# A state-space scan, an attention and an expert layer on one core: the product with B in two halves, the product with C behind a semaphore, the last columns on VectorE, the gate on y's banks, and a new order of the work

## The chip, the cores and the metric

The kernel runs on one core of a Trainium2 chip. The metric is the device time of one execution in microseconds; the median of several runs is given. Engines are called PE (TensorE), DVE (VectorE), ACT (ScalarE), POOL (GpSimd) and SP (SyncE, which here only issues DMAs).

## The reference

The input `x` has 16 images of 128 channels and 64 x 64 pixels. Layer 0 is a group norm, then a selective state-space block over the 4096 tokens of an image with 256 inner channels and 16 states, and a residual. Layer 1 is a causal softmax-weighted attention with one query per head (8 heads), and then a layer of 64 experts that each choose 8 tokens. The change touches layer 0 and, in small things, the attention's scores. Cut to what matters:

```python
u = x.transpose(0, 2, 3, 1).reshape(b, h * w, c)
xs, z = jnp.split(u @ W_in, 2, axis=-1)
xc = silu(causal_depthwise_conv4(xs) + conv_b)
dt, Bm, Cm = jnp.split(xc @ W_xproj, [DT_RANK, DT_RANK + D_STATE], axis=-1)
delta = softplus(dt @ W_dt + b_dt);  A = -exp(A_log)
def step(hs, inp):
    d_t, B_t, C_t, u_t = inp
    h_new = exp(d_t[:, :, None] * A) * hs + (d_t * u_t)[:, :, None] * B_t[:, None, :]
    y_t = einsum('bdn,bn->bd', h_new, C_t)
    return h_new, y_t
y = (scan(step) + xc * D_param) * silu(z)
out = y @ W_out
# attention: s = q . silu(k);  exp(s - cummax(s)), its running sum u, the running sum w of exp(...) * silu(v);  w / u, mean of heads
```

## The kernel before

**Tiling.** Channels lie on the 128 partitions, tokens along the free dimension. An image is cut into 8 blocks of 512 tokens, so there are 128 blocks. The 256 inner channels are two halves `a` of 128 partitions; a tile such as `h` is 128 x 2 x 512 in fp32. One loop over `k` runs the scan of block `k`, the preparation of block `k + 1` (norm, convolution, projections, `delta`), the closing of block `k - 1` (gate, output projection, residual) and the attention of block `k - 9`, all interleaved. After the loop come ten rounds with attention alone, then the choice of tokens, the experts, and a last pass that adds their outputs.

**The state loop.** In block `k` there is one step for each state `n` from 0 to 15:

- `product` (line 379): DVE multiplies `du` (delta times the convolved input) by row B of `bct`, a tile in which both rows (B and C) of this state are spread over all partitions by a DMA on SP three steps earlier. The result `bx` (128 x 1024) is in PSUM, in one tile with one buffer.
- `scan` (line 385): two `tensor_tensor_scan` on DVE, one for each half, read the decay `da` (made by ACT ahead of time) and `bx` and write `h`; the start value is the kept `state` of the block before. Then POOL multiplies `h` by row C and writes over `da`.
- `keep_state` (line 406): POOL copies the last column of both halves of `h` (two elements per partition) to `state`, except in an image's last block.
- `add_pair` (line 401): for n = 1, 3, 5, 7 POOL issues a DMA that adds the `da` of the state before into this one.
- `add_y` (line 412): PE transposes `da` and accumulates it in `y` (two PSUM banks, one buffer) with tokens on partitions.

**The closing of a block.** `take_y` has ACT copy `y` to SBUF, `turn_y` has PE turn it back to channels on partitions (`yb`), `gate` has DVE multiply it with `z`, and `out_proj` has PE multiply by `wo`.

**Order.** Every engine works through its instructions in program order (`InOrder`, line 22). The interleaving is written out by hand: `STEP` (line 724) has for each `n` three strings of short names, and `do(n, part)` (line 831) issues them: part 0 after `product`, part 1 between the two scans (through `between`), part 2 after the state is kept. A `d` issues one decay. `ge0` to `ge4` are the parts of `gn_end` (line 258), which ends the group norm's statistics of the next image; `less` is `score_less` (line 533), six small DVE operations on the attention's scores; `gate0` and `gate1`, `takey`, `turny`, `outp`, `put` close the block; `du` makes `delta_x` of the next block; `ar0` to `ar3` and `sr0` to `sr3` add the residual by DMAs on POOL and store it by DMAs on SP.

Of the kernel before, what the change touches and what calls it, by code (L numbers as in the profile page):

```python
# [17 lines left out]
NEG = -3.0e38  # L18
OFF = -1.0e30
EXP_LN = "natural_log_exp_and_others"  # L20


class InOrder:
# [16 lines left out]
def conv_attn_hybrid(ctx: ExitStack, tc: tile.TileContext, x, w_in, conv_w, conv_b, w_xproj, w_dt, b_dt,  # L40
# [41 lines left out]
    with ExitStack() as st:  # L82
# [175 lines left out]
        def gn_end(b, part):  # L258

            w = gn[b]  # L260
            if part == 0:
                w["mv"] = stp.tile([P, 2], F32, tag="mv", name="mv")
                w["gs"] = stp.tile([P, 5], F32, tag="gs", name="gs")
                DVE.bn_aggr(w["mv"], w["stats"].rearrange("p a b -> p (a b)"))
            mv, gs = w["mv"], w["gs"]
            if part == 1:
                w["gp"] = bank("gn_ps")
                PE.matmul(w["gp"][:, 0:1], gmat, mv[:, 0:1], start=True, stop=True)
                ACT.copy(gs[:, 0:1], w["gp"][:, 0:1])
            if part == 2:  # L270
                DVE.tensor_tensor(gs[:, 1:2], mv[:, 0:1], gs[:, 0:1], ALU.subtract)
                DVE.scalar_tensor_tensor(gs[:, 1:2], gs[:, 1:2], gs[:, 1:2], mv[:, 1:2], ALU.mult, ALU.add)
            if part == 3:
                w["gp"] = bank("gn_ps2")
                PE.matmul(w["gp"][:, 0:1], gmat, gs[:, 1:2], start=True, stop=True)
                ACT.activation(gs[:, 2:3], w["gp"][:, 0:1], AF.Ln, bias=eps)
                ACT.activation(gs[:, 3:4], gs[:, 2:3], AF.Exp, scale=-0.5)
            if part == 4:
                DVE.tensor_scalar(gs[:, 4:5], gs[:, 0:1], gs[:, 3:4], -1.0, ALU.mult, ALU.mult)
# [35 lines left out]
                ACT.activation(xc[:, a, :], w[f"xs{a}"], AF.Silu, bias=cb[:, a : a + 1])  # L315

        def gate_silu(k):
            w = blocks[k]
            z = w["z"] = m1.tile([P, NH2, L], F32, tag="z", name="z")
            for a in range(NH2):  # L320
                pt = bank("z_ps")
                PE.matmul(pt, wz[:, bass.ts(a, P)], w["xb"][:, KC - 1 :], start=True, stop=True)
                ACT.activation(z[:, a, :], pt, AF.Silu)

        def xproj(k):

# [52 lines left out]
        def product(k, n):  # L379

            w = blocks[k]
            bx = w["bx"] = bps.tile([P, NH2, L], F32, tag="bx", name="bx")
            DVE.tensor_tensor(bx, w["du"], bc(w["bc", n][:, 0:1, :], [P, NH2, L]), ALU.mult)

        def scan(k, n, between):


            w = blocks[k]
            b, i = w["b"], w["i"]
            if n == 0 and i == 0:  # L390
                gn[b]["state"] = stp.tile([P, N, NH2], F32, tag="state", name="state")
            bt, da, bx = w.pop(("bc", n)), w["da", n], w.pop("bx")
            h = w["h", n] = hp_.tile([P, NH2, L], F32, tag="h", name="h")
            for a in range(NH2):
                if a:
                    between(n)
                DVE.tensor_tensor_scan(h[:, a, :], da[:, a, :], bx[:, a, :],
                                       0.0 if i == 0 else gn[b]["state"][:, n, a : a + 1], ALU.mult, ALU.add)
            POOL.tensor_tensor(da, h, bc(bt[:, 1:2, :], [P, NH2, L]), ALU.mult)

        def add_pair(k, n):

# [3 lines left out]
        def keep_state(k, n):  # L406
            w = blocks[k]
            h = w.pop(("h", n))
            if w["i"] < NBLK - 1:
                POOL.tensor_copy(gn[w["b"]]["state"][:, n, :], h[:, :, L - 1])  # L410

        def add_y(k, n):

# [11 lines left out]
                              is_transpose=True, skip_group_check=True)  # L425


        def take_y(k):
            w = blocks[k]
            yt = w["yt"] = a1.tile([P, L // P, DI], F32, tag="wm", name="yt", bufs=2)  # L430
            for c in range(0, L // P, 2):
                ACT.copy(yt[:, c : c + 2, :], w["y"][:, c : c + 2, :])

        def turn_y(k):
            w = blocks[k]
            for a in range(NH2):
                yb = w[f"yb{a}"] = bank("yb_ps")
                for c in range(L // P):
                    PE.transpose(yb[:, bass.ts(c, P)], w["yt"][:, c, bass.ts(a, P)], ident)

        def gate(k, a):
            w = blocks[k]
            DVE.tensor_tensor(w["z"][:, a, :], w[f"yb{a}"], w["z"][:, a, :], ALU.mult)

        def tokens_of(w):

# [3 lines left out]
        def out_proj(k):  # L450

            w = blocks[k]
            w["o"] = bank("o_ps")
            for a in range(NH2):
                PE.matmul(w["o"], wo[:, a, :], w["z"][:, a, :], start=(a == 0), stop=(a == NH2 - 1))

        def add_residual(b, part):

# [3 lines left out]
                POOL.dma_start(res[b][:, to], x_f[b, :, to], accum_op=ALU.add)  # L462

        def store_residual(b, part):
            SP.dma_start(t1_d[b, :, bass.ts(part, T // 4)], res[b][:, bass.ts(part, T // 4)])

        def put_back(k):
            w = blocks.pop(k)
# [61 lines left out]
            s["mx"] = a1.tile([P, 64], F32, tag="mx", name="mx")  # L530
            DVE.tensor_tensor_scan(s["mx"], bc(negc, [P, 64]), s["s"][:, :64], NEG, ALU.max, ALU.max)

        def score_less(m):


            i = m % NBLK
            s = att[m]
            mx, z = s.pop("mx"), s["s"][:, 64:P]
            DVE.transpose(z[:, 32:], mx[:, 32:])
            if i == 0:  # L540
                DVE.memset(z[:, 0:48:47], NEG)
            else:
                DVE.tensor_copy(z[:, 0:48:47], zl)
            DVE.tensor_tensor_scan(z[:, 1:32], open_, z[:, 32:63], z[:, 0:1], ALU.min, ALU.max)
            DVE.tensor_copy(zl, z[:, NC8 : NC8 + 17 : 16])
            back = stp.tile([P, 32], F32, tag="back", name="back")
            DVE.transpose(back, z[:, :32])
            s["x2"] = a1.tile([P, 2, 64], F32, tag="x2", name="x2")
            DVE.scalar_tensor_tensor(s["x2"][:, 0, :], mx, back[:, 31:32], s["s"][:, :64], ALU.max, ALU.subtract)

        def score_exp(m):
            s = att[m]
# [161 lines left out]
        def finish(m, f):  # L714
# [7 lines left out]
        PAIRS = (1, 3, 5, 7)  # L722
        LEAD, LEAD_BC = 8, 3
        STEP = (
            ("lx0 k0 k4 yp14", "yp15", "takey k1 k2"),
            ("k3 v6", "norm skip", "tu0 fin0"),
            ("", "k5", "ge0 s0 k6 turny ge1 k7"),
            ("s1", "gate0", ""),
            ("v4 v7 ge2 gate1 v5 mx d d y-1 conv0", "d less y1", "sexp"),
            ("w1 a10 a11 exp d ts1", "ge3 outp d put tsc ssp c1 d", ""),  # L730
            ("", "", "conv1"),
            ("ar0 ssum ar1 b1 d slog rest1 ar2 split1 y3 to1 rest2 d conv2 csilu", "split2", "d store v0"),
            ("tu1 lx1 v2 ge4", "fin1 cen", ""),
            ("", "", ""),
            ("v1 xproj v3 z delta sq exp bcs", "var", "lnsc"),
            ("", "y5 y7", "spread inv w0 d"),
            ("gnl a00 a01", "y8", "d y9 lb ar3 sr0"),
            ("sr1 d y10 y11 ts0 d", "c0 y12", ""),
            ("b0", "", "sr2"),
            ("d lnap gns", "du", "nt d d sr3 y13 d d to0"),  # L740
        )
        order = [(k, n) for k in range(NK) for n in range(N)]
        made = 0
# [35 lines left out]
        for k in range(NK + LAG + 1):  # L779
# [11 lines left out]
            ops = dict(  # L791
                norm=(nxt, norm_block), conv0=(nxt, lambda k: conv(k, 0)), conv1=(nxt, lambda k: conv(k, 1, range(KC // 2))),
                conv2=(nxt, lambda k: conv(k, 1, range(KC // 2, KC))), csilu=(nxt, conv_silu), xproj=(nxt, xproj),
                bcs=(nxt, store_bc), delta=(nxt, delta), du=(nxt, delta_x), z=(cur, gate_silu), skip=(cur, skip),
                takey=(prev, take_y), turny=(prev, turn_y), gate0=(prev, lambda k: gate(k, 0)),
                gate1=(prev, lambda k: gate(k, 1)), outp=(prev, out_proj), put=(prev, put_back),
                cen=(mn, ln_center), sq=(mn, ln_square), var=(mn, ln_var), lnsc=(mn, ln_scale), lnap=(mn, ln_apply),
                mx=(m, score_max), less=(m, score_less), sexp=(m, score_exp), tsc=(m, turn_scores), ssum=(m, score_sum),
                ssp=(m, spread_scores), slog=(m, score_log), rest1=(m, lambda m: rest(m, 1)), split1=(m, lambda m: split(m, 1)),
                rest2=(m, lambda m: rest(m, 2)), split2=(m, lambda m: split(m, 2)), store=(m, store_parts),  # L800
                spread=(m, spread_parts), inv=(m, inverse), lx0=(mn, lambda m: load_x(m, True)), lx1=(m, load_x),
                gnl=(stat, lambda s: gn_load(*s)), gns=(stat, lambda s: gn_stats(*s)),
                lb=(k + 2 if k + 2 < NK else None, lambda k: load_block(k, ACT)),
                nt=(k + 2 if k + 2 < NK else None, no_tokens), exp=(0, lambda _: load_exp()))
            for h in range(HD):
# [13 lines left out]
            for f in range(2):  # L819
                ops[f"tu{f}"] = (mp_, lambda m, f=f: turn_o(m, f))  # L820
                ops[f"fin{f}"] = (mp_, lambda m, f=f: finish(m, f))
            for n in range(-1, N):
                ops[f"y{n}"] = (cur, lambda k, n=n: add_y(k, n))
                ops[f"yp{n}"] = (prev, lambda k, n=n: add_y(k, n))
# [13 lines left out]
                        f(of)  # L838

            for n in range(N):  # L840
                if cur is not None:
                    product(cur, n)
                do(n, 0)
                if cur is not None:
                    later = k * N + n + LEAD_BC
                    if later < NK * N:
                        load_bc(*order[later])
                    scan(cur, n, lambda n: do(n, 1))
                    keep_state(cur, n)
                    if n in PAIRS:  # L850
                        add_pair(cur, n)
                else:
                    do(n, 1)
                do(n, 2)
# [292 lines left out]
```

## Time and profile before

| | |
|---|---|
| median of 3 runs | 9924.13 us (9919.84 to 9943.96) |
| profiled execution | 9941.12 us, its span 9939.4 us |
| busy in the span | PE 86%, DVE 88%, ACT 74%, POOL 73%, PE weight loads 51% |
| scans on DVE | 4096, together 5022 us |
| products with B on DVE | 2048, 2621 us, mean 1280 ns |
| products with C on POOL | 2048, 6626 us, mean 3240 ns |
| copies of the last columns on POOL | 1792, 432 us |

The profile is of one execution. Times in it are microseconds unless ns is said. A line of the timeline has start, duration, engine, the line of the code, operation, names and shapes (out<-in), and how many in a row. All engines but PE share one line, 31, because a helper issues their work, so groups are told apart by the names of their tiles. A busy share is an average over the whole span; the scan stage runs from about 50 us to 8680 us.

### The profile page before, as it was taken

To read this page: it belongs to the slowest core of one execution; us is meant where nothing else is said; L and a number is where in the kernel's file an instruction comes from. 1 tells how busy PE (TensorE), PEld (TensorE's weight loads), DVE (VectorE), ACT (ScalarE), POOL (GpSimd) and SP (SyncE) were. 2 spreads that over 40 slices of the span, in tenths; PEclk is the share of its full clock that TensorE was granted. 3 is DMA by queue.
4 is the path that set the end of the run, shared out by engine and by line. 5 is a ranking of instruction groups with operands and counts; after the bars stand their busy time and mean duration, and the time that the engine had idled before them with its cause. 6 is when DMAs were issued, how large, how long until landed. Compare 5 with 4: busy or idle time off the path is not lost.

```text
span 9939.4 us, 183919 instructions
## 1 busy us (share of the span) xinstructions
PE 8516.5 (86%) x69084; PEld 5113.5 (51%) x69084; DVE 8709.0 (88%) x9217; ACT 7385.9 (74%) x14079; POOL 7301.8 (73%) x4475
## 2 busy tenths in 40 slices
PE   5579898998989898989999898989898998877775
PEld 3345555555555555555555555555555555545642
DVE  8999999999999999999999999999999999902743
ACT  4568787888878887878878788878788887755730
POOL 7888888888888888888888888888888888800000
PEclk7789999999999999999999999999999999998976
DMA  6677777777776777777777777777777777611358
GB/s 164 173 188 181 189 185 190 183 179 192 181 194 176 197 181 189 182 191 180 186 190 177 194 181 193 180 194 178 194 181 192 183 178 186 163 38 55 119 169 352
DMA packets 978014, 1783.42 MB, mean 179 GB/s; under 512 B 194953, under 2 KB 275489, under 8 KB 967905
## 3 DMA queue, kind: packets, MB, share of 16 engines
q1 hardware_dynamic: 724480, 1381.32, 50.1%
q0 software_dynamic: 82944, 302.03, 15.4%
q10 hardware_dynamic: 169696, 88.30, 3.1%
q8 instruction: 544, 8.91, 0.3%
q14 instruction: 350, 2.86, 0.1%
HBM read 1363.99 MB, written 138.94 MB: 151 GB/s over the span
## 4 chain that ended last, share of the span: by engine, by line
PE 45%; ACT 34%; DVE 9%; DMA 6%; issue 5%; ACTq 1%; SPq 0%; POOL 0%; DVEq 0%; POOLq 0%
ACT da L31 11%; PE ao_ps L31 9%; PE v_ps L31 9%; PE y_ps L31 6%; ACT L31 6%; PE k_ps L31 4%; DVE h L31 3%; DVE bx L31 3%; PE o_ps L31 2%; PE z_ps L31 2%; ACT xc L31 2%; PE xs_ps L31 2%; PE var_ps L31 2%; ACT kt L31 2%; DMA bct<-bcs 2%
## 5 line engine op out<-in xcount | busy, mean ns | idle before, releaser
L31 POOL TENSOR_TENSOR da<-h,bct 128x1024 f32<-128x1024 f32 x2048 | 6626.3, 3240 | 1275.8 <-DVE h L31 667.0
L31 DVE TENSOR_TENSOR_SCAN h<-da,state,bx 128x512 f32<-128x512 f32 x3584 | 4420.8, 1267 | 201.6 <-DVE bx L31 4.3
L31 DVE TENSOR_TENSOR bx<-du,bct 128x1024 f32<-128x1024 f32 x2048 | 2621.4, 1280 | 115.0 <-DMA bct<-bcs 45.8
L31 ACT ACTIVATE da<-delta,a_neg 128x512 f32<-128x512 f32 x4096 | 2621.8, 714 | 27.9 <-DMA da<-da 17.2
L31 PE MATMUL y_ps<-ident,da 128*128 128x128 f32 x12288 | 1708.5, 296 | 236.6 <-POOL da L31 124.5
L31 PEld LDWEIGHTS y_ps<-ident,da 128*128 128x128 f32 x12288 | 1559.7, 154 | 540.8 <-issue 256.3
L31 PE MATMUL v_ps<-wv,xn 128*64 128x512 f32 x4096 | 1074.6, 624 | 200.3 <-ACT xc L31 134.9
L31 ACT ACTIVATE v<-v_ps 128x512 f32<-128x512 f32 x1024 | 610.8, 598 | 790.6 <-PE v_ps L31 790.0
L31 PE MATMUL k_ps<-xn,wk 128*128 128x512 f32 x2048 | 1038.7, 613 | 97.6 <-ACT kt L31 93.1
L31 PE MATMUL xs_ps<-xb,wc 128*128 128x512 f32 x2048 | 975.7, 609 | 23.7 <-ACT xt L31 4.2
L31 ACT ACTIVATE kt<-k_ps 128x512 f32<-128x512 f32 x1024 | 565.6, 612 | 234.2 <-PE k_ps L31 165.0
L31 PE MATMUL ao_ps<-v,wm 128*64 128x128 f32 x8192 | 580.4, 286 | 151.9 <-ACT wm L31 150.7
L31 ACT ACT_TABLE_LOAD x526 | 674.9, 1283 | 14.1 <-ACT parts L31 4.4
L31 DVE TENSOR_TENSOR_SCAN h<-da,bx 128x512 f32<-128x512 f32 x512 | 600.8, 1208 | 32.5 <-POOL state L31 3.0
L31 PEld LDWEIGHTS v_ps<-wv,xn 128*64 128x64 f32 x4096 | 228.5, 137 | 745.6 <-ACT xc L31 232.4
L31 PEld LDWEIGHTS ao_ps<-v,wm 128*64 128x64 f32 x8192 | 453.8, 140 | 267.4 <-ACT wm L31 213.5
L31 PEld LDWEIGHTS xs_ps<-xb,wc 128*128 128x128 f32 x2048 | 366.0, 193 | 368.8 <-issue 321.7
L31 POOL DMA_DIRECT2D da<-da x512 | 460.0, 899 | 98.4 <-POOL state L31 65.4
L31 PEld LDWEIGHTS k_ps<-xn,wk 128*128 128x128 f32 x2048 | 331.2, 190 | 349.4 <-ACT kt L31 215.6
L31 PE MATMUL var_ps<-sq,mean_w 128*128 128x512 f32 x256 | 219.6, 953 | 277.8 <-ACT sq L31 277.8
L31 POOL COPY state<-h 128x2 f32<-128x2 f32 x1792 | 432.4, 241 | 0.0
L31 PEld LDWEIGHTS s_ps<-kt,q 128*32 128x32 f32 x16384 | 257.2, 110 | 271.6 <-issue 97.8
(209 smaller groups left out, 10326.6 us busy)
## 6 DMA issues: line engine op xcount, KB each, us to landing
bct<-bcs SPq DMA_DIRECT2D x2048, 512.0 KB
da<-da POOLq DMA_DIRECT2D x512, 512.0 KB, 7.9
xs<-t_d SPq DMA_DIRECT2D x240, 256.0 KB
xs<-in_x_dram SPq DMA_DIRECT2D x128, 256.0 KB
t_d<-xt SPq DMA_DIRECT2D x64, 512.0 KB
t_d<-tx ACTq DMA_DIRECT2D x256, 128.0 KB
t<-t_d SPq DMA_DIRECT2D x128, 256.0 KB
tc<-t_d SPq DMA_DIRECT2D x16, 2048.0 KB
```

What stands on the lines that cost most here:

```text
L31: return lambda *args, **kw: self.tc.keep_in_program_order(f(*args, **kw))
```

## The change

- `product` writes two PSUM tiles `bx0` and `bx1` with two DVE instructions of 128 x 512.
- The product with C and the pair's DMA leave `scan`; a new function `product_c` issues them in the next step, after that step's `product`, and makes POOL wait by a semaphore for that step's first half (in the last step of a block, for its second half, behind which `delta_x` of the next block is issued at once).
- `keep_state` runs there too, on DVE in place of POOL.
- The gate multiplies `y` in PSUM, tokens on partitions, with a `z` that is now made with tokens on partitions; only then PE turns the result and ACT copies it out (`gy`), and `out_proj` reads `gy`.
- In part 2 of `gn_end` the intermediate value lies in PSUM (`far`).
- `score_less` comes in six parts `l0` to `l5`. The residual's stores are issued on ACT's queue. `STEP` is new.

```diff
+def after(tc, ins, other):
+    tc.add_manual_dep(ins.ins, other.ins.name,
+                      mybir.DependencyInfo(mybir.DependencyClass.Sync, mybir.DependencyReason.DATA), reason="port")
 def gn_end(b, part):
             if part == 2:
-                DVE.tensor_tensor(gs[:, 1:2], mv[:, 0:1], gs[:, 0:1], ALU.subtract)
-                DVE.scalar_tensor_tensor(gs[:, 1:2], gs[:, 1:2], gs[:, 1:2], mv[:, 1:2], ALU.mult, ALU.add)
+                far = w["gp"][:, 1:2]
+                DVE.tensor_tensor(far, mv[:, 0:1], w["gp"][:, 0:1], ALU.subtract)
+                DVE.scalar_tensor_tensor(gs[:, 1:2], far, far, mv[:, 1:2], ALU.mult, ALU.add)
...
 def gate_silu(k):
-            z = w["z"] = m1.tile([P, NH2, L], F32, tag="z", name="z")
-            for a in range(NH2):
+            z = w["z"] = m1.tile([P, L // P, DI], F32, tag="z", name="z")
+            for q in range(2):
                 pt = bank("z_ps")
-                PE.matmul(pt, wz[:, bass.ts(a, P)], w["xb"][:, KC - 1 :], start=True, stop=True)
-                ACT.activation(z[:, a, :], pt, AF.Silu)
+                for c in range(2):
+                    at = KC - 1 + (2 * q + c) * P
+                    PE.matmul(pt[:, bass.ts(c, DI)], w["xb"][:, at : at + P], wz, start=True, stop=True)
+                ACT.activation(z[:, 2 * q : 2 * q + 2, :].rearrange("p c d -> p (c d)"), pt, AF.Silu)
...
 def product(k, n):
-            bx = w["bx"] = bps.tile([P, NH2, L], F32, tag="bx", name="bx")
-            DVE.tensor_tensor(bx, w["du"], bc(w["bc", n][:, 0:1, :], [P, NH2, L]), ALU.mult)
+            bx = w["bx"] = [bps.tile([P, L], F32, tag=f"bx{a}", name=f"bx{a}") for a in range(NH2)]
+            for a in range(NH2):
+                w["bxi", a] = DVE.tensor_tensor(bx[a], w["du"][:, a, :], w["bc", n][:, 0, :], ALU.mult)
...
-            POOL.tensor_tensor(da, h, bc(bt[:, 1:2, :], [P, NH2, L]), ALU.mult)
+            w["hc", n] = bt
+        def product_c(k, n, behind):
+            w = blocks[k]
+            bt = w.pop(("hc", n))
+            ins = POOL.tensor_tensor(w["da", n], w["h", n], bc(bt[:, 1:2, :], [P, NH2, L]), ALU.mult)
+            if behind is not None:
+                after(tc, ins, behind)
+            if n in PAIRS:
+                add_pair(k, n)
...
-                POOL.tensor_copy(gn[w["b"]]["state"][:, n, :], h[:, :, L - 1])
+                DVE.tensor_copy(gn[w["b"]]["state"][:, n, :], h[:, :, L - 1])
...
-        def take_y(k):
-        def gate(k, a):
-            DVE.tensor_tensor(w["z"][:, a, :], w[f"yb{a}"], w["z"][:, a, :], ALU.mult)
+        def gate(k, q):
+            cs = slice(2 * q, 2 * q + 2)
+            DVE.tensor_tensor(w["z"][:, cs, :], w["y"][:, cs, :], w["z"][:, cs, :], ALU.mult)
+        def turn_y(k, a):
+            if a == 0:
+                w["gy"] = a1.tile([P, NH2, L], F32, tag="wm", name="gy", bufs=2)
+            yb = bank("yb_ps")
+            for c in range(L // P):
+                PE.transpose(yb[:, bass.ts(c, P)], w["z"][:, c, bass.ts(a, P)], ident)
+            ACT.copy(w["gy"][:, a, :], yb)
...
-            SP.dma_start(t1_d[b, :, bass.ts(part, T // 4)], res[b][:, bass.ts(part, T // 4)])
+            ACT.dma_start(t1_d[b, :, bass.ts(part, T // 4)], res[b][:, bass.ts(part, T // 4)])
...
+            ("yp14 yp15 k4 ge0 k0", "", "k1 k2"),
+            ("k3", "k5", ""),
+            ("norm tu0 g0 ge1 g1 fin0", "", "s0 v6 k6 k7"),
+            ("", "", "ty0 s1 ty1 skip"),
+            ("v7 v4 lx0 mx v5 exp y-1 l1 d d ge2 l0", "y1 w1 d d l2 l4 l3 l5", "conv0"),
+            ("d sexp d d ge3 a10 outp a11", "", "tsc"),
+            ("ssp y3", "", "put ts1"),
+            ("ssum slog conv1 rest1 d d c1 split1 conv2 rest2 csilu", "split2", "d b1"),
+            ("", "ar0 lx1 store z v2 to1 xproj v0 tu1", ""),
+            ("", "ge4 ar1 bcs v3", ""),
+            ("cen fin1 sq v1 delta var exp lnsc y5 ar2", "", ""),
+            ("inv", "", "ar3 spread"),
+            ("sr0 d y7 y8 w0 d d", "a00", "y9 d"),
+            ("a01 ts0 lb y10", "sr1 y11 d", "c0"),
+            ("d sr2 gnl la", "nt d y12", ""),
+            ("y13 b0", "gs", "sr3 d to0"),
...
             for n in range(N):
+                behind = None
                 if cur is not None:
                     product(cur, n)
+                    behind = blocks[cur]["bxi", 0]
+                    if n == N - 1 and nxt is not None:
+                        behind = blocks[cur]["bxi", 1]
+                        delta_x(nxt)
+                if 0 < k * N + n <= NK * N:
+                    product_c(*divmod(k * N + n - 1, N), behind)
+                    keep_state(*divmod(k * N + n - 1, N))
                 do(n, 0)
...
                     scan(cur, n, lambda n: do(n, 1))
-                    keep_state(cur, n)
-                    if n in PAIRS:
-                        add_pair(cur, n)
```

More of the change, by code (lines that the diff above doesn't have):

```diff
@@ L396, in scan @@
                     between(n)
-                DVE.tensor_tensor_scan(h[:, a, :], da[:, a, :], bx[:, a, :],
+                DVE.tensor_tensor_scan(h[:, a, :], da[:, a, :], bx[a],
                                        0.0 if i == 0 else gn[b]["state"][:, n, a : a + 1], ALU.mult, ALU.add)
-            POOL.tensor_tensor(da, h, bc(bt[:, 1:2, :], [P, NH2, L]), ALU.mult)
+            w["hc", n] = bt
[7 more added lines that the diff above has]
+                add_pair(k, n)
         def add_pair(k, n):
@@ L425, in add_y @@
                               is_transpose=True, skip_group_check=True)
-        def take_y(k):
+        def gate(k, q):
             w = blocks[k]
[L430 to L434, printed above, removed]
+            cs = slice(2 * q, 2 * q + 2)
+            DVE.tensor_tensor(w["z"][:, cs, :], w["y"][:, cs, :], w["z"][:, cs, :], ALU.mult)
+        def turn_y(k, a):
             w = blocks[k]
[L436 to L439, printed above, removed]
-        def gate(k, a):
-            w = blocks[k]
-            DVE.tensor_tensor(w["z"][:, a, :], w[f"yb{a}"], w["z"][:, a, :], ALU.mult)
+            if a == 0:
[4 more added lines that the diff above has]
+            ACT.copy(w["gy"][:, a, :], yb)
         def tokens_of(w):
@@ L454, in out_proj @@
             for a in range(NH2):
-                PE.matmul(w["o"], wo[:, a, :], w["z"][:, a, :], start=(a == 0), stop=(a == NH2 - 1))
+                PE.matmul(w["o"], wo[:, a, :], w["gy"][:, a, :], start=(a == 0), stop=(a == NH2 - 1))
         def add_residual(b, part):
@@ L531, in score_max, with score_less @@
             DVE.tensor_tensor_scan(s["mx"], bc(negc, [P, 64]), s["s"][:, :64], NEG, ALU.max, ALU.max)
-        def score_less(m):
+        def score_less(m, part):
             i = m % NBLK
             s = att[m]
[L538 to L549, printed above, removed]
+            mx, z = s["mx"], s["s"][:, 64:P]
+            if part == 0:
+                DVE.transpose(z[:, 32:], mx[:, 32:])
+            if part == 1:
+                if i == 0:
+                    DVE.memset(z[:, 0:48:47], NEG)
+                else:
+                    DVE.tensor_copy(z[:, 0:48:47], zl)
+            if part == 2:
+                DVE.tensor_tensor_scan(z[:, 1:32], open_, z[:, 32:63], z[:, 0:1], ALU.min, ALU.max)
+            if part == 3:
+                DVE.tensor_copy(zl, z[:, NC8 : NC8 + 17 : 16])
+            if part == 4:
+                s["back"] = stp.tile([P, 32], F32, tag="back", name="back")
+                DVE.transpose(s["back"], z[:, :32])
+            if part == 5:
+                s["x2"] = a1.tile([P, 2, 64], F32, tag="x2", name="x2")
+                DVE.scalar_tensor_tensor(s["x2"][:, 0, :], mx, s["back"][:, 31:32], s["s"][:, :64], ALU.max, ALU.subtract)
         def score_exp(m):
@@ L724, in conv_attn_hybrid @@
         STEP = (
[L725 to L740, printed above, removed]
+            ("yp14 yp15 k4 ge0 k0", "", "k1 k2"),
[10 more added lines that the diff above has]
+            ("inv", "", "ar3 spread"),
[4 rows of a table added]
         )
@@ L793, in conv_attn_hybrid @@
                 conv2=(nxt, lambda k: conv(k, 1, range(KC // 2, KC))), csilu=(nxt, conv_silu), xproj=(nxt, xproj),
[L794 to L798, printed above, removed]
+                bcs=(nxt, store_bc), delta=(nxt, delta), z=(cur, gate_silu), skip=(cur, skip),
+                outp=(prev, out_proj), put=(prev, put_back),
+                cen=(mn, ln_center), sq=(mn, ln_square), var=(mn, ln_var), lnsc=(mn, ln_scale),
+                mx=(m, score_max), sexp=(m, score_exp), tsc=(m, turn_scores), ssum=(m, score_sum),
                 ssp=(m, spread_scores), slog=(m, score_log), rest1=(m, lambda m: rest(m, 1)), split1=(m, lambda m: split(m, 1)),
@@ L801, in conv_attn_hybrid @@
                 spread=(m, spread_parts), inv=(m, inverse), lx0=(mn, lambda m: load_x(m, True)), lx1=(m, load_x),
-                gnl=(stat, lambda s: gn_load(*s)), gns=(stat, lambda s: gn_stats(*s)),
+                gnl=(stat, lambda s: gn_load(*s)),
                 lb=(k + 2 if k + 2 < NK else None, lambda k: load_block(k, ACT)),
@@ L821, in conv_attn_hybrid @@
                 ops[f"fin{f}"] = (mp_, lambda m, f=f: finish(m, f))
+            for q in range(2):
+                ops[f"g{q}"] = (prev, lambda k, q=q: gate(k, q))
+            for a in range(NH2):
+                ops[f"ty{a}"] = (prev, lambda k, a=a: turn_y(k, a))
+            ops["la"] = (mn, ln_apply)
+            ops["gs"] = (stat, lambda s: gn_stats(*s))
+            for part in range(6):
+                ops[f"l{part}"] = (m, lambda m, part=part: score_less(m, part))
             for n in range(-1, N):
```

## The prediction

> **What bounds the kernel now.** I read the page's busy table first, then the slices of busy time, then the timeline of VectorE (DVE) and GpSimd (POOL) in one steady block, then single tiles.
>
> ```profile
> PE 8516.5 (86%) x69084; PEld 5113.5 (51%) x69084; DVE 8709.0 (88%) x9217; ACT 7385.9 (74%) x14079; POOL 7301.8 (73%) x4475
> DVE  8999999999999999999999999999999999902743
> 4019.18:4085.28 66.10, 60.23 (x501) 35.51 (x500) 63.19 (x60) 54.67 (x103) 56.56 (x36) 0.95 0.72 181
> ```
>
> The third line is one block of 512 tokens (window, its length, then busy us of PE, weight loads, DVE, ACT, POOL): DVE 63.19 of 66.10 us. Across 1000 to 8000 us it is 6675 of 7000. The scan stage lasts to 8.7 ms, so DVE's instruction starts, added up, are the time. The chain of waits names PE and ACT (45% and 34%), but it ran last through the attention tail after 8.7 ms; in the stage DVE hardly waits for them.
>
> A plain step of the state loop (start, duration, DVE):
>
> ```profile
> 4056.87 1.23 DVE L31 TENSOR_TENSOR bx<-du,bct 128x1024 f32<-128x1024 f32 x1
> 4058.24 2.45 DVE L31 TENSOR_TENSOR_SCAN h<-da,state,bx 128x512 f32<-128x512 f32 x2
> 4060.72 1.23 DVE L31 TENSOR_TENSOR bx<-du,bct 128x1024 f32<-128x1024 f32 x1
> ```
>
> Start to start: product to first scan 1.37, scans to the next product 2.48, together 3.85 us. The block's end shows what the same instructions cost when the next one does not depend on them:
>
> ```profile
> 4013.23 1.23 DVE L31 TENSOR_TENSOR bx<-du,bct 128x1024 f32<-128x1024 f32 x1
> 4014.37 0.69 DVE L31 TENSOR_TENSOR xn<-cen_ps,rstd 128x512 f32<-128x512 f32 x1
> 4014.97 0.68 DVE L31 BATCH_NORM_STATS2 stats<-xs 128x6 f32<-128x512 f32 x1
> 4015.57 1.26 DVE L31 TENSOR_TENSOR_SCAN h<-da,state,bx 128x512 f32<-128x512 f32 x1
> 4016.76 1.20 DVE L31 TENSOR_TENSOR du<-delta,xc 128x1024 f32<-128x1024 f32 x1
> 4039.73 0.16 DVE L31 COPY zl<-s_ps 128x2 f32<-128x2 f32 x1
> 4039.81 0.20 DVE L31 STREAM_TRANSPOSE back<-s_ps 128x32 f32<-128x32 f32 x1
> ```
>
> A product of 1024 costs 1.14, an operation of 512 costs 0.60, a scan 1.20 (1.19 to 1.20), a two-element copy 0.08. So a step holds about 0.23 us of waiting for the product and 0.08 for the scan before it (both use one `bx` tile).
>
> [...]
>
> ```profile
> 453.20 1.23 DVE L31 TENSOR_TENSOR bx<-du,bct 128x1024 f32<-128x1024 f32 x1
> 454.35 2.31 DVE L31 TENSOR_TENSOR gs<-mv,gs 128x1 f32<-128x1 f32 x1
> 456.69 0.22 DVE L31 SCALAR_TENSOR_TENSOR gs<-gs,mv 128x1 f32<-128x1 f32 x1
> 453.25 3.39 POOL L31 TENSOR_TENSOR da<-h,bct 128x1024 f32<-128x1024 f32 x1 [0.93 <-DVE h L31]
> ```
>
> POOL's product C is issued at 453.25, waits for `bx` (ends 454.43), then runs 2.21 us to 456.64. `gs<-mv,gs`, one element with two SBUF inputs, queued right behind `bx`, gets in only then. So **at the end of a DVE product, a waiting POOL beats the next DVE instruction**, in 15 of 16 such cases (median 2322 ns against a least of 160).
>
> [...] This bears on the new copy of last columns (two elements, step 512). The trace has no such copy. The nearest row is `gs<-gs`, a one-source SBUF operation of one element, also right behind a `bx` with POOL waiting: 205 to 213 ns each time, so it does not wait. [...]
>
> **The change, part by part** (per step or block of the scan stage).
>
> *Product in two halves.* New step: 0.60 + 0.60 for the halves, 1.20 + 1.20 for the scans, 0.08 for the copy now on DVE: 3.68 against 3.85, gain 0.17. The first scan needs only half 0, which ends at 0.68, before half 1 is through at 1.28. Two of 16 steps already had other work behind the product (n = 4 and 15: 2.48 + 1.14 = 3.62), and lose 0.06. A block gains 14 x 0.17 - 2 x 0.06 = 2.26; 128 blocks, 289 us. The last block of each image copies nothing: 256 x 0.08 = 20 more. Sum **-309**.
>
> *Hold on product C.* POOL waits for half 0 (ends 0.68 into the step), arrives near 0.8[...], runs 2.21 and is done at 3.49, 0.19 before the next half 0. Before, it was done about 3.4 into its step, so `y` gets its input no later. Behind it on POOL are the pair DMA (0.88, ends 4.37; next release near 4.45) and the residual DMAs (1.13 each, 64 in all). PE's `y` transposes wait for it. At n = 15 half 1 releases it[...]. By itself 0; if POOL is late, each 0.1 over the 0.19 costs 0.1 a step, 205 us in all. It does prevent a backlog of two POOL products from stopping `bx`: the mean of `bx` is 1280 and the median 1233, 47 ns x 2048 = 96 us, of which I take two thirds: **-65**, bounds -96 and 0.
>
> *Copy off POOL.* 1792 copies leave POOL (432 us, not binding). Their price on DVE is in the step: 0.08 by the `zl` row, bounds 0.08 and[...] 2.2 each. I take 0.08.
>
> *Group statistics through PSUM.* One SBUF input instead of two: 15 x (2.32 - 0.16) = **-32**; bounds -35 and 0.
>
> *Gate on y's banks.* Two DVE operations of 512, two ACT copies, eight transposes before and after. The wait for `yb_ps` (43.1 us in all) goes; late next would be the last `y` transposes, given some 3 us by step 2. **-30**, bounds -43 and +20. The z matmuls keep their columns (2 x 512 against 4 x 256), with two more weight loads a block at about 0.19: +0.4 us of PE loads, beside other matmuls.
>
> *Score operations apart.* Six small DVE operations ran in a row in 1.28 us (4038.97 to 4040.25), each waiting for the last; interleaved, near 1.05: **-25** over 128 blocks, bounds -35 and +10.
>
> *Residual stores* move 64 DMA issues from SP to ACT. ACT is busy 54.67 of 66.10 us, and an issue takes 0.36 on SP (the loads of `bct`), so 0, at most 64 x 0.36 = 23. SP's loads of `bct`, which keep their place three steps ahead of their product, no longer stand behind a store that waits for `res`.
>
> *New order.* PE is busy 60.2 us a block. At 63 it has 2.8 spare instead of 5.9, and its queue is in order, so some waits come through to DVE: **+50** (0.4 a block), bounds 0 and 360 (all of the gain).
>
> Sum: 309 + 65 + 32 + 30 + 25 - 50 = 411. The profiled execution took 9941 in all (span 9939), so 9530; the median of the runs stands 17 below it: **9510**. Its own range: 9400 to 9700.
>
> **Rivals.**
>
> [...] It follows half 1 directly on DVE's queue, where POOL has been waiting since 0.8. That is the situation of `gs<-mv,gs`, and POOL wins. Then 1.28 + 2.21 = 3.49 before the copy, 2.36 for the scans behind it: 5.85 a step, +2.00 x 1792 = 3584. The 256 steps without a copy gain 0.25 (64), the other savings stand (152), PE has time: 9941 + 3584 - 216 = 13309, less 17, **13290** (13100 to 13400). [...] Against it: the only small one-source SBUF operation seen in this place passes[...]. [...] The gain of 411 / 128 = 3.2 us a block is gone once 3.2 / 2.2 = 1.5 of a block's 16 copies are stopped.
>
> *PE becomes the bound.* If its queue can't go under 65 us a block, 1.1 is gained on 119 blocks (131) and perhaps 100 of the rest: 9941 - 231 - 17 = **9690**. For it: 60.2 busy; against it: PE's idle is a few large waits (2.2, 1.2 and 0.9 us in the block at 4019) that a new order can shift.
>
> *The hold costs.* If POOL starts over 0.19 late, the next half 0 waits; the gain is eaten at 0.36, near 9900. Against it: POOL's arrival at 0.8 has 0.48 of half 1 as cover.
>
> *The hold does nothing.* POOL could then enter between the halves and stop half 1, the price of the first rival. A semaphore wait is explicit, so hardly.
>
> **How the numbers follow.** No change can be told within 0.3%, 30 us. Forecast 0.51; PE bound 0.08; [...] the hold costs or does nothing 0.04. Faster: 0.51 + 0.08 + 0.01 = 0.60; within 0.3% 0.03; slower 0.37. Cases of both signs hold most of the chance, and 2 in 10 can't be left out without the first rival: the range goes from 9400 to 13400, beside 9400 to 9700 of the likeliest.
>
> **What would show it.** Right: `bx` twice as often at about 0.68, product to scans 1.20, steps of 3.68, blocks near 63; `state<-h` on DVE at 0.16; `gs<-mv` at 0.2; POOL's product ending 3.5 into the step. Wrong: `state<-h` at some 2.3 us with POOL's product inside it and steps of 5.85 (first rival); DVE idle before `z`, `mx` or `xn` for PE (second); halves over 0.68 (third).

## The result, and the profile after

The changed kernel takes 13,147.56 us (median of 4 runs, 13,146.49 to 13,157.75), against 9,923.82 before: a ratio of 1.3245, 95% interval 1.3222 to 1.3268. It is **slower by 3,224 us**. My likeliest case, 9,510, was wrong; the time fell in the range of the first rival (the copy waits for POOL; 13,100 to 13,400), priced at 13,290.

The page of the changed kernel: busy time of each engine, DVE's busy tenths, and the group of the copies (busy, mean ns).

```profile
PE 9267.9 (70%) x69596; PEld 5745.3 (44%) x69596; DVE 12264.6 (93%) x13057; ACT 7297.8 (55%) x13950; POOL 5920.2 (45%) x2683
DVE  9999999999999999999999999999999999991362
L37 DVE COPY state<-h 128x2 f32<-128x2 f32 x1792 | 4103.9, 2290 | 0.0
```

DVE "busy" went up by 3,556 us; one group that was not on DVE before, copies of two elements, takes 4,104 alone. PE, ACT and POOL all have a smaller share of the span: nothing else came near being the bound. A plain step on DVE, and POOL's product in it (start, duration):

```profile
5007.43 1.27 DVE L37 TENSOR_TENSOR bx<-du,bct 128x512 f32<-128x512 f32 x2
5008.61 2.30 DVE L37 COPY state<-h 128x2 f32<-128x2 f32 x1
5010.83 2.44 DVE L37 TENSOR_TENSOR_SCAN h<-da,state,bx 128x512 f32<-128x512 f32 x2
5013.19 1.27 DVE L37 TENSOR_TENSOR bx<-du,bct 128x512 f32<-128x512 f32 x2
5008.33 2.56 POOL L37 TENSOR_TENSOR da<-h,bct 128x1024 f32<-128x1024 f32 x1 [3.20 <-DVE bx L37]
```

Read it in order of time. The halves start at 5007.43 and end at 5008.70. POOL's product was released by half 0 and is issued at 5008.33, while half 1 runs. The copy is issued at 5008.61 and ends at 5010.91, just after POOL's product at 5010.89. The scans wait behind the copy. The step is 5.76 us in place of 3.85. It is so nearly everywhere: read instruction by instruction, 1,769 of the 1,792 copies take over 1 us, and in 1,768 of these POOL's product was issued before the copy. The copy's record begins at 5008.61, before half 1 has ended, and covers the wait, so **this wait looks like a long instruction and not like idle time**: 2315 ns at the median against a least of 151, and the column of idle time says 0.0.

The same kernel has blocks without copies (the last of each image). Two steps of one:

```profile
5187.43 1.28 DVE L37 TENSOR_TENSOR bx<-du,bct 128x512 f32<-128x512 f32 x2
5190.97 1.27 DVE L37 TENSOR_TENSOR bx<-du,bct 128x512 f32<-128x512 f32 x2
```

There the plain steps take 3.55 us and the blocks 64.5 us at the median, from first product to first product (one copy, of the block before, is still in their first step), against 97.5 for most others and 66.1 for the same blocks before. So the halves do shorten the step, and the copy adds 2.2 us to it.

### The profile page after: what moved, and what is told of

Its sections match the earlier page's. It is cut to its first block, busy times and chain, and to the rows that moved or that the text cites. A ratio compares the mean times of both kernels' runs of the same rounds, so it can differ in the third digit from the quotient of the medians.

```text
span 13156.1 us, 189003 instructions
## 1 busy us (share of the span) xinstructions
PE 9267.9 (70%) x69596; PEld 5745.3 (44%) x69596; DVE 12264.6 (93%) x13057; ACT 7297.8 (55%) x13950; POOL 5920.2 (45%) x2683
## 4 chain that ended last, share of the span: by engine, by line
DVE 42%; issue 24%; PE 14%; DMA 9%; ACT 6%; POOL 3%; SPq 1%; ACTq 0%; DVEq 0%; POOLq 0%
DVE h L37 26%; DVE bx L37 8%; DVE state L37 5%; DMA bct<-bcs 4%; POOL da L37 3%; PE k_ps L37 3%; PE y_ps L37 2%; PE ao_ps L37 2%; DMA da<-da 2%; PE v_ps L37 1%; ACT xn L37 1%; ACT da L37 1%; PE f_ps L1155 1%; DVE z L37 1%; PE s_ps L37 1%
## 5 line engine op out<-in xcount | busy, mean ns | idle before, releaser
L37 POOL TENSOR_TENSOR da<-h,bct 128x1024 f32<-128x1024 f32 x2048 | 5413.6, 2643 | 5809.4 <-DVE bx L37 4013.8
L37 DVE TENSOR_TENSOR_SCAN h<-da,state,bx 128x512 f32<-128x512 f32 x3584 | 4389.1, 1259 | 0.0
L37 DVE COPY state<-h 128x2 f32<-128x2 f32 x1792 | 4103.9, 2290 | 0.0
L37 PE MATMUL y_ps<-ident,da 128*128 128x128 f32 x12288 | 2050.2, 330 | 1824.6 <-POOL da L37 1410.5
L37 ACT ACTIVATE da<-delta,a_neg 128x512 f32<-128x512 f32 x4096 | 2618.2, 713 | 268.2 <-DMA bct<-bcs 101.4
L37 PEld LDWEIGHTS y_ps<-ident,da 128*128 128x128 f32 x12288 | 1766.6, 172 | 2174.6 <-POOL da L37 1519.7
L37 DVE TENSOR_TENSOR bx<-du,bct 128x512 f32<-128x512 f32 x4096 | 2603.2, 679 | 2.0 <-DMA bct<-bcs 2.0
L37 PE MATMUL v_ps<-wv,xn 128*64 128x512 f32 x4096 | 1159.1, 668 | 1135.9 <-ACT v L37 1010.8
L37 ACT ACTIVATE v<-v_ps 128x512 f32<-128x512 f32 x1024 | 593.1, 596 | 1703.9 <-DMA bct<-bcs 1304.6
L37 ACT ACTIVATE kt<-k_ps 128x512 f32<-128x512 f32 x1024 | 607.3, 597 | 1579.6 <-PE k_ps L37 1509.8
L37 PE MATMUL k_ps<-xn,wk 128*128 128x512 f32 x2048 | 1063.6, 667 | 0.0
L37 PE MATMUL xs_ps<-xb,wc 128*128 128x512 f32 x2048 | 1044.0, 646 | 1.9 <-issue 1.8
L37 PEld LDWEIGHTS v_ps<-wv,xn 128*64 128x64 f32 x4096 | 249.8, 145 | 1531.9 <-ACT v L37 1108.2
L37 PE MATMUL ao_ps<-v,wm 128*64 128x128 f32 x8192 | 590.8, 289 | 125.6 <-ACT wm L37 125.5
L37 PEld LDWEIGHTS k_ps<-xn,wk 128*128 128x128 f32 x2048 | 427.6, 221 | 551.8 <-issue 403.6
L37 DVE TENSOR_TENSOR_SCAN h<-da,bx 128x512 f32<-128x512 f32 x512 | 595.9, 1198 | 0.0
L37 PEld LDWEIGHTS ao_ps<-v,wm 128*64 128x64 f32 x8192 | 461.2, 142 | 296.7 <-ACT wm L37 159.4
L37 PEld LDWEIGHTS xs_ps<-xb,wc 128*128 128x128 f32 x2048 | 403.6, 213 | 379.3 <-issue 373.1
L37 POOL DMA_DIRECT2D da<-da x512 | 449.3, 878 | 163.4 <-POOL da L37 155.3
L37 ACT COPY gy<-yb_ps 128x512 f32<-128x512 f32 x256 | 149.8, 585 | 438.1 <-PE yb_ps L37 437.4
```

The lines of the kernel that those rows point to most:

```text
L37: return lambda *args, **kw: self.tc.keep_in_program_order(f(*args, **kw))
```

## The experiments

**The theories.** A: POOL's product is already waiting when half 1 ends and runs first, and the copy of two elements, which does not depend on it, waits for the whole product. B: the copy waits for POOL through an ordinary dependence on a tile. C: the copy is slow by itself, through its step of 512 elements.

**Release POOL later.** The copy stays as it is (`delta_x` now returns its instruction).

```diff
-                    behind = blocks[cur]["bxi", 0]
+                    behind = blocks[cur]["bxi", 1]
                     if n == N - 1 and nxt is not None:
-                        behind = blocks[cur]["bxi", 1]
-                        delta_x(nxt)
+                        behind = delta_x(nxt)
```

> The changed kernel, but POOL's product with C is released by the last DVE instruction[...]: half 1, and at n = 15 delta_x. The copy of the last columns stays on DVE, in its place and form. Theory A[...]: now the copy (done near 1.30 us into the step) is through before POOL arrives at 1.37, so state<-h falls from 2.3 to about 0.16 us; POOL's product runs undisturbed from 1.37 for 2.35 and ends at 3.72, which now sets the step: about 3.72 us, 9,650 to 9,850 in all. Theory B (the copy waits for POOL through an ordinary dependence, a semaphore on da, h or state): moving the release later makes it wait longer, steps of 6 us, 13,300 or more. Theory C (the copy of two elements at a step of 512 is slow by itself): no change, about 13,150.

Measured: 9,702.74 us, ratio to the kernel before 0.9773 (0.9755 to 0.9791). The timeline of DVE and POOL:

```profile
5004.47 0.15 DVE L37 COPY state<-h 128x2 f32<-128x2 f32 x1
5004.54 2.44 DVE L37 TENSOR_TENSOR_SCAN h<-da,state,bx 128x512 f32<-128x512 f32 x2
5006.90 1.40 DVE L37 TENSOR_TENSOR bx<-du,bct 128x512 f32<-128x512 f32 x2
5004.78 2.36 POOL L37 TENSOR_TENSOR da<-h,bct 128x1024 f32<-128x1024 f32 x1 [1.39 <-DVE state L37]
```

The same copy, with the same step of 512, takes 0.15 us and holds the scan up by 0.07 once POOL comes after it. B and C fall. POOL's product now ends at 5007.14, and the halves that start at 5006.90 take 1.40 in place of 1.27: POOL's round (about 3.75 a step) is the limit, as expected, and the time lies in the range expected for A.

**Two copies of one element.** POOL is released by half 0 as in the changed kernel. A copy of one element may pass, or the first of the two may wait as the copy of two elements does.

```diff
-                DVE.tensor_copy(gn[w["b"]]["state"][:, n, :], h[:, :, L - 1])
+                for a in range(NH2):
+                    DVE.tensor_copy(gn[w["b"]]["state"][:, n, a : a + 1], h[:, a, L - 1 : L])
```

> The changed kernel, with the copy of two elements (128x2) made two copies of one element each (128x1), on DVE, same place, same release of POOL by half 0. Theory A[...]: [...] each costs about 0.08 to 0.16 us, steps of 3.55 + 0.16 = 3.71 to 3.85, 9,650 to 9,950 in all. [...] the first of the two waits 2.2 us and nothing is gained: about 13,200. Theory B: about 13,200. Theory C (a slow step of 512): two copies of one element have no step, so fast too.

Measured: 9,607.14 us, ratio 0.9680 (0.9666 to 0.9695). The tile `state` (duration min/median/max in ns), and a step beside POOL:

```profile
L37 DVE COPY state<-h x3584: 130/145/159, 56.6 to 8276.9; 128x1 f32<-128x1 f32 x200
...
5004.22 0.20 DVE L37 COPY state<-h 128x1 f32<-128x1 f32 x2
5004.35 2.43 DVE L37 TENSOR_TENSOR_SCAN h<-da,state,bx 128x512 f32<-128x512 f32 x2
5003.93 2.58 POOL L37 TENSOR_TENSOR da<-h,bct 128x1024 f32<-128x1024 f32 x1 [1.08 <-DVE bx L37]
```

None of 3,584 copies waits, although POOL's product stands in the same place as in the changed kernel: in the step shown it was issued 0.29 us ahead of the pair. The step is 3.67 us, and the time lies a little below the range expected. Whether a copy waits for POOL is a matter of its form, not of copying: 159 ns at most with one element, 2315 at the median with two.

**Which form waits.** Two copies of two neighbouring columns each, and two of three each, in place of one element each; the scan reads the last. Three elements may pass as one does, or wait as two do.

```diff
+                for a in range(NH2):
+                    DVE.tensor_copy(gn[w["b"]]["state"][:, n, a, :], h[:, a, L - 2 : L])   # L - 3 in the other
```

> The changed kernel, with the one copy of two elements (128x2, step 512) made two copies of two neighbouring elements each (128x2, step 1), one for each half; the scan reads the second. Theory A[...]: the first copy waits for POOL's product as in the changed kernel, about 13,100 to 13,250. If it was the step of 512, or the mere presence of one copy instead of two: as with two single elements, about 9,600.

> The changed kernel, with two copies of three neighbouring elements each (128x3, step 1); the scan reads the third. [...] as with single elements, about 9,600. [...] the first copy waits 2.2 us, about 13,100 to 13,250. I expect the latter at 6 in 10.

Measured: 13,330.33 and 13,329.24 us (one run each, so without an interval), some 80 above the ranges named for a copy that waits. The tile `state` of the two, pairs first:

```profile
L37 DVE COPY state<-h x3584: 152/1228/3000, 55.5 to 12004.7; 128x2 f32<-128x2 f32 x200
```

```profile
L37 DVE COPY state<-h x3584: 152/1229/3005, 55.3 to 12006.6; 128x3 f32<-128x3 f32 x200
```

A median of 1228 between two values: read instruction by instruction, the first of each two copies has a median of 2.32 us and the second of 0.15. Neighbouring elements wait as elements 512 apart do, and three wait as two do. Of 1, 2 and 3 elements, only the copy of one passes (145 ns at the median).

**The copy alone on the kernel before.** No halves, no semaphore, old order.

```diff
-                POOL.tensor_copy(gn[w["b"]]["state"][:, n, :], h[:, :, L - 1])
+                DVE.tensor_copy(gn[w["b"]]["state"][:, n, :], h[:, :, L - 1])
...
                 if cur is not None:
                     product(cur, n)
+                if 0 < k * N + n <= NK * N:
+                    keep_state(*divmod(k * N + n - 1, N))
                 do(n, 0)
...
-                    keep_state(cur, n)
```

> The kernel before, with one edit: the copy of the last columns goes from POOL to DVE, right behind the next step's whole product. No halves, no hold, old order. Theory A[...]: POOL is issued 0.1 us into the product, waits for its end (1.23), runs 2.21 to 3.44 and the copy waits for that: steps of 5.8 to 5.9 instead of 3.85, state<-h at 2.3 us, about 13,500 in all. If the stall needs the halves or the semaphore of the changed kernel: steps near 3.9, 9,900 to 10,050.

Measured: 13,353.95 us (one run). DVE, then POOL:

```profile
5004.72 1.23 DVE L31 TENSOR_TENSOR bx<-du,bct 128x1024 f32<-128x1024 f32 x1
5005.86 2.32 DVE L31 COPY state<-h 128x2 f32<-128x2 f32 x1
5004.83 3.33 POOL L31 TENSOR_TENSOR da<-h,bct 128x1024 f32<-128x1024 f32 x1 [1.35 <-DVE h L31]
```

POOL is issued 0.11 us behind the product and ends at 5008.16; the copy ends at 5008.18. The stall needs neither halves nor semaphore: this one edit makes the kernel slower by a third (about 13,500 was expected).

**Copy on POOL.** Back where it was, right behind the product with C and ahead of the pair's DMA; the rest of the change stays.

```diff
 def product_c(k, n, behind):
...
+            keep_state(k, n)
             if n in PAIRS:
                 add_pair(k, n)
...
-                DVE.tensor_copy(gn[w["b"]]["state"][:, n, :], h[:, :, L - 1])
+                POOL.tensor_copy(gn[w["b"]]["state"][:, n, :], h[:, :, L - 1])
...
-                    keep_state(*divmod(k * N + n - 1, N))
```

> The changed kernel, with the copy of the last columns back on POOL, right behind the product with C and ahead of the pair's DMA. Theory A: DVE no longer competes in the middle of the step, but POOL's product ends at 3.49 of a step of 3.55 and the copy (0.18) reads SBUF until 3.65, so the next half 0 waits about 0.1: steps of 3.6 to 3.75, 9,450 to 9,750 in all. If POOL's late copy costs more than its own time, 9,800 to 10,000.

Measured: **9,485.46 us, ratio 0.9555 (0.9541 to 0.9570)**, the fastest version of this study and faster than both kernels. Steps are 3.55 us. The price expected for POOL's copy behind its product is hardly there:

```profile
5000.84 1.28 DVE L37 TENSOR_TENSOR bx<-du,bct 128x512 f32<-128x512 f32 x2
5004.39 1.28 DVE L37 TENSOR_TENSOR bx<-du,bct 128x512 f32<-128x512 f32 x2
5001.75 2.57 POOL L37 TENSOR_TENSOR da<-h,bct 128x1024 f32<-128x1024 f32 x1 [0.84 <-ACT v L37]
5004.27 0.18 POOL L37 COPY state<-h 128x2 f32<-128x2 f32 x1
```

POOL's copy ends at 5004.45, 0.06 after half 0 was issued, and the halves take 1.28 instead of 1.27.

**The same without the hold.** The variant with the copy on POOL, but POOL's product may start as soon as `h` is complete (the dependence on `h` stays).

```diff
-            if behind is not None:
-                after(tc, ins, behind)
```

> The variant with the copy back on POOL (9,485 us), but without the semaphore on the first half: POOL's product may start as soon as h is complete. Theory A[...]: POOL arrives 0.1 us into half 0, gets in at its end, and half 1 waits 2.2 us: bx mean near 1.8 us (half of them 0.68, half some 2.9), steps of 5.8, about 14,000 in all. If [...] the hold does nothing: steps of 3.55 and about 9,485.

Measured: 13,464.42 us (one run). DVE, then POOL:

```profile
5007.90 3.44 DVE L37 TENSOR_TENSOR bx<-du,bct 128x512 f32<-128x512 f32 x2
5008.12 2.66 POOL L37 TENSOR_TENSOR da<-h,bct 128x1024 f32<-128x1024 f32 x1 [2.85 <-PE s_ps L37]
```

Read instruction by instruction, half 0 has a median of 669 ns and half 1 of 2843. POOL was issued at 5008.12, while half 0 ran; the record of half 1 begins at 5008.48, so it came second and waited. So the hold does what the change says, and is worth some 4,000 us once the product is cut in two. The copy fell into the trap that the hold avoids for half 1. I expected 14,000; the step was 5.70 at the median and not 5.8.

**Copy on ACT.** First with the changed kernel's two buffers of `h`, then with three.

```diff
-                DVE.tensor_copy(gn[w["b"]]["state"][:, n, :], h[:, :, L - 1])
+                ACT.copy(gn[w["b"]]["state"][:, n, :], h[:, :, L - 1])
...
-        hp_ = st.enter_context(tc.tile_pool(name="hp", bufs=2))
+        hp_ = st.enter_context(tc.tile_pool(name="hp", bufs=3))      # in the second only
```

> The changed kernel, with the copy of the last columns on ACT in place of DVE, same place in the program. Theory A: [...] steps fall to the 3.55 us that the changed kernel shows in the blocks without copies; blocks near 62, 9,370 to 9,500 in all, faster than the kernel before by some 5%. If PE or the new order bounds the kernel once the copy is gone: blocks at 64 to 66, 9,700 to 9,950. Theory B: the copy waits on ACT instead, ACT's decays come late, over 12,000.

Measured: 10,233.62 us, ratio 1.0309 (1.0293 to 1.0324). All three of my numbers missed. The waits of this variant, and then of one with three buffers of `h` in place of two:

```profile
DVE h L37 <- ACT state L37: 750.8, 519, 8.7
```

> The variant with the copy on ACT (10,234 us), with three buffers of h in place of two. In that variant DVE's scans waited 750 us for ACT's copies, since h has two buffers and the copy stands in ACT's queue behind work that waits for PE. If this is the cause: most of the 750 us go, 9,450 to 9,650. If ACT is late in itself: 10,100 to 10,250.

```profile
DVE h L37 <- ACT state L37: 497.0, 312, 12.6
```

Measured with three buffers: 9,787.54 us, ratio 0.9871 (0.9849 to 0.9894). 446 us go, as much as DVE's idle time before its scans falls by, whatever ended it (959 to 499 us). But 497 us of waiting for ACT's copies stay. ACT works in program order: its copy stands behind other ACT work, and the buffer of `h` is not free until it has run. That this work waits for PE is likely but not shown to be what counts here. The gain is short of what I expected; more buffers were not tried.

**The loop's part alone on the kernel before.** Halves, hold, and POOL's copy behind the product with C, with the old gate, group statistics, score operations, stores and order. `product` and `product_c` are those of the change, the latter with `keep_state` on POOL.

```diff
+                behind = None
                 if cur is not None:
                     product(cur, n)
+                    behind = blocks[cur]["bxi", 0]
+                if 0 < k * N + n <= NK * N:
+                    product_c(*divmod(k * N + n - 1, N), behind)
                 do(n, 0)
```

> The kernel before with the loop's part alone: product in two halves, product with C held until the next first half, the copy staying on POOL behind the product with C. Gate, group statistics, score operations, residual stores and order as before. Theory A: steps of 3.55 instead of 3.85; a block gains 14 x 0.30 + 2 x 0.07 = 4.3 us if nothing else stops it, 9,390 in all. If the old order leaves PE or the gate late (43 us of waits before): 9,450 to 9,700. The variant of the whole change with the copy on POOL took 9,485; the difference is what the new order and the small parts give.

Measured: 9,889.14 us, ratio 0.9971 (0.9961 to 0.9981); 9,390 missed, and so did the range beside it. Steps did fall to 3.55, yet only some 30 us came, and a block takes 66.7 us at the median, against 66.6 before. DVE's waits of this variant, and one of them in the timeline:

```profile
DVE z L37 <- PE yb_ps L37: 509.7, 118, 14.1
```

```profile
5003.55 0.69 DVE L37 TENSOR_TENSOR z<-yb_ps,z 128x512 f32<-128x512 f32 x1 [4.35 <-PE yb_ps L37]
```

Before, that wait was 43.1 us in all. DVE now reaches the gate some 4 us a block before PE has turned `y` back, and gives back what the steps saved. PE itself hardly got faster. Its transposes to `yb_ps` in two blocks that follow each other, of the kernel before (L31) and of this variant (L37):

```profile
4033.14 0.60 PE L31 MATMUL yb_ps<-ident,yt 128*128 128x128 f32 x4
4100.13 1.40 PE L31 MATMUL yb_ps<-ident,yt 128*128 128x128 f32 x8
5002.91 1.40 PE L37 MATMUL yb_ps<-ident,yt 128*128 128x128 f32 x8
5068.98 1.40 PE L37 MATMUL yb_ps<-ident,yt 128*128 128x128 f32 x8
```

They are 66.99 and 66.07 us apart. Between 5000 and 5070 us of this variant the chain of waits (the work that ended last, followed back to what released it) holds work of PE and ACT and none of DVE. In the block at 4019 us of the kernel before it does so too. So in the old order PE and ACT, releasing each other, need about as long for a block as DVE does, and shorter steps on DVE alone gain little. This is read from the traces; the new order alone was not run. In the variant with the copy on POOL, which has the same steps, the gate's wait for `y` is 3.8 us in all.

**The group statistics alone, and with the loop's part.** The edit is that of the change's diff.

> The kernel before with the group statistics' intermediate value in PSUM alone: gs<-mv,gs with two SBUF inputs waited 2.32 us for POOL 15 times, a one-element operation takes 0.16. Expected 15 x 2.16 = 32 us less, 9,890. If the waiting only moves to another operation: 9,920.

> Both of the above on the kernel before: the loop's part and the group statistics through PSUM. If the parts add up: about 30 us below the kernel with the loop's part alone, 9,360 to 9,650.

Measured: 9,909.83 us, ratio 0.9990 (0.9984 to 0.9997), and 9,866.41 us, ratio 0.9951 (0.9934 to 0.9968). The operation of the first variant:

```profile
453.44 0.16 DVE L31 TENSOR_TENSOR gn_ps<-mv,gn_ps 128x1 f32<-128x1 f32 x1
```

It fell from 2.31 to 0.16 us as forecast, but about 9 of the expected 32 us arrived. Together the two gained 53 us; the sum of their single gains, 39, lies within the interval. Where the other 23 us went was not settled; the wait for `yb_ps` grew from 43.1 to 53.9 us in this variant, which would be half of it and fits the chain of PE and ACT above.

## Why the prediction was wrong

- **The step that failed is "Copy off POOL".** I took 0.08 us from the `zl` row, whose source is in PSUM, and gave the other bound, 2.2 us, 37 in 100. It measured 2290 ns at the mean and 2.2 in the step. The trace of the kernel before gave one half of the argument: a waiting POOL wins at the end of a DVE product (15 of 16 cases of `gs<-mv,gs`, 2322 ns at the median against a least of 160). That a copy of two elements from SBUF to SBUF would lose as well was an assumption that no row of that trace shows, and I let the row `gs<-gs` (205 to 213 ns) speak against it. That row has one element; it says nothing of two, and the runs show the border exactly there: one passes (130 to 159 ns), two and three wait (2.3 us at the median). The step did not matter for these copies: 512 and 1 behave alike (2315 ns and 2.32 us). The runs show which copies wait for POOL; why these forms do was not shown.
- **The rival's price** was 13,290 against 13,148. Its terms: the step 5.85 against 5.76 to 5.80, on 1,792 steps some 90 to 160 us. POOL's product ran as assumed (2.2 us behind half 1).
- **The gain of the product in two halves** was undersized for the step and oversized for the kernel. I put a half at 0.60 and a scan at 1.20; the step without copy is 3.55, not 3.60. But the loop's part alone gave 30 us, where I had booked 309 for the halves. A copy of two elements that POOL does not hold up costs the 0.07 to 0.08 that I took (5004.47 to 5004.54 with POOL released later).
- **The hold** at 0 by itself: right. POOL, released by half 0, is done in time for steps of 3.55, with 0.07 us to spare in the step shown of the version with the copy on POOL. The rival that the hold does nothing is refuted by the run without it. The -65 for products that POOL stops is not separated: no half takes over 0.71 us in the changed kernel, but the longest is 3.6 us in the version with the copy on POOL.
- **Gate and new order** were mis-sized most after the copy. I booked -30 for the gate and +50 for PE. The runs with the copy on POOL show that the gain depends on these parts: 9,889 without gate, order and small parts, 9,485 with them. DVE's wait for `y` is what differs most (510 us against 4). In the changed kernel ACT also loads its tables 677 times in place of 806, at 1.28 us each. Which of the parts does it was not separated, and the score operations and the stores were not run alone.
- **PE as the bound** did not decide the changed kernel, but my reading of what bounds the kernel before was incomplete. I put the chain of PE and ACT down to the attention's tail; it runs through the very block that I showed, and the loop's part alone stops at it. In the version with the copy on POOL, DVE waits 260 us for the scores from PE (`mx`, 170 before) and 249 for ACT's `rstd` ahead of `xn` (173 before).
- **Group statistics**: the operation as forecast, the saving 9 in place of 32. What took the rest is open.
- **The nearness of 9,485** (the copy on POOL) to my 9,510 is partly luck: its step is 0.13 shorter than the 3.68 that I booked and has no copy on DVE, and the parts that I put at -30 and +50 decide whether the steps count at all.

The loss in one sum: 1,792 copies at 2.2 us are 3,940 us; the version with the copy on POOL is 437 us faster than before; 3,940 - 437 = 3,503, against 3,224 measured. Of the rest, 280 us, some 196 are waits for PE, ACT and DMA that the fast version has and the slow one hides behind its stall (DVE's waits at `mx`, `xn` and for `bct` are 84, 50 and 62 us longer in it). The remaining 84 were not traced.

## What to carry to other kernels

Before you move a small operation to VectorE while GpSimd works beside it, measure its form in the place where it will stand, and ask what GpSimd has already waiting when it is issued; a small operation is not safe for being small, since here a copy of two elements waited 2.2 us for a whole GpSimd product and one of one element took 0.15. Such a wait shows as a long instruction, so look for a median far above the shortest of the same form (2315 ns against 151 here). And when a faster loop gains less than its steps say, look at the first instruction that takes another engine's result: here the gate gave back 510 us as long as the old gate and order stood. Ask for the chain of waits inside the stage, too: a second chain as long as the first shows there.

## What the runs showed of the hardware

- A DVE copy from SBUF to SBUF in fp32 that was issued behind a waiting GpSimd product with two SBUF inputs waited for that product with 2 elements per partition (2315 ns median at a step of 512, 2.3 us at a step of 1) and with 3 (2.3 us); with 1 it did not (130 to 159 ns in 3,584 cases). ACT's copies of two elements took 187 ns at the mean of 1,792.
- A GpSimd product that was issued during the first half of a DVE product ran between the halves: their records have medians of 669 and 2843 ns.
- Being issued first did not always decide. In the kernel before, a DVE product issued at 1688.93, while a POOL product ran, took 4.27 us (1.23 at the median) and ended at 1693.20: the next POOL product, issued at 1689.04, ended before it, at 1692.11.
- Two DVE products of 128x512 that do not depend on each other started 0.58 us apart (median of 2,048 pairs in the changed kernel), and a product in two halves with two scans took 3.55 us where one product of 1024 with two scans took 3.85.
